# Layer 1's attention in other turns: sums of weights on quarter columns, byte masks, results turned back together

## The chip, the cores and the metric

The kernel runs on one core of one Trainium2 chip. The metric is the device time of one execution in microseconds (us). A smaller time is better. The engines are TensorE (matrix products, PE in the profile; PEld is its loading of weights), VectorE (DVE), ScalarE (ACT), GpSimd (POOL) and SyncE (SP), which here only issues DMAs.

## What is computed

The reference takes `x` of 32 x 512 x 256 and an adjacency `adj` of 32 x 512 x 512 with entries 0 and 1, and applies two layers. Each layer is a graph step and a feed-forward step, both added to `x` after a layer norm. The change lies in the graph step of layer 1, an attention with 4 heads of 64 values:

```python
h = jnp.einsum('bnd,hde->bhne', nodes_embed, W)
e_src = jnp.einsum('bhne,hte->bhtn', h, a_src)
e_dst = jnp.einsum('bhne,hte->bhtn', h, a_dst)
for t in range(n_types):
    mask = (node_adj == t + 1).astype(h.dtype)[:, None]
    weight = weight + mask * (e_src[:, :, t, :, None] + e_dst[:, :, t, None, :])
weight = jax.nn.leaky_relu(weight, negative_slope=0.01)
weight = jnp.where(node_adj[:, None] == 0, NEG, weight)
attention = jax.nn.softmax(weight, axis=-1)
dst = jnp.einsum('bhij,bhje->bhie', attention, h) + bias[None, :, None, :]
out = jax.nn.relu(dst) + h
```

The result is normalised per head, scaled and added to `x`. The feed-forward step of layer 1, called the mixer below, weighs all tokens into 64 slices, runs a short scan over the slices and spreads the result back over the tokens.

## The kernel before

An image `b` (32 of them) has 512 tokens, in NT = 4 tiles of P = 128 tokens. AH = 4 heads form AP = 2 pairs `q`; HO = 64 values make up a head.

Layer 0 runs first and takes somewhat more than half of the time. Layer 1 (`layer1_plain`) has three parts as Python generators, which are advanced step by step, so that their instructions alternate in each engine's queue. The order in which instructions are issued is fixed at build time.

`prepare(b)` brings an image in. GpSimd gathers its rows into `x` (L1075; five buffers, so that it waits for the store of an image five before), SyncE loads the adjacency tile by tile (`ai`, L1084). ScalarE turns a tile into bf16 (`a`, L1092) and sums squares (L1093). `turn_edges` (L1146 on) transposes a tile on TensorE into PSUM (`maskp`) and VectorE copies it into `mask` (L1151). Then come the layer norm (`hv`), its transpose (`x3T`), the product with the weights (`hp`, L1121), and exponentials on ScalarE, which are finished so that attention needs only a maximum and a product. The terms of the other side are brought to all partitions by four DMAs into `own` (L1141).

`attention(b)` goes through eight turns, pair by pair and within a pair over the four tiles `j` of neighbours: (0,0), (0,1), (0,2), (0,3), (1,0) and so on. `weigh` makes a turn's two tiles of weights `att` on VectorE (L1160: the larger of `own` and `other`, times `mask`), three turns (AHEAD) before TensorE uses them. A turn then has four f32 matmuls (L1199), each with 512 moving elements per partition. Two of them multiply the two heads' values (`avp`): head k of the pair goes to PSUM partitions 64k to 64k+63, hence to that half of the array's columns. The other two multiply a column that holds a factor of the weights' sum, repeated 64 times, by the same weights (`adp`), again on half of the columns each. They give every head the sum it has to be divided by, 64 equal rows of it.

After a pair's last turn ScalarE copies `adp` and `avp` to SBUF (`adT`, `avT`, L1205 and L1206). `back` (L1169 on) transposes both, four 128 x 128 pieces each (`dp`, `bp`, L1175), and VectorE divides (`rs`, L1177 and L1178; `av`, L1179). For the first pair this comes one turn later, in the middle of the image. `norm` (L1228 on) does the per-head normalisation of an image during the first turns of the next.

The mixer `mixer(g)` takes a group of two images: `slices` (exponentials of `lgp`, sums `yTp`, transposes `swp`), `tokens` (`uTp`, `rnp`), `scan` (`xp`, `bcp`, `dtp`, `zp`, then `gp`, `segp`, `xtp`, `yp`, `qp`, `yTp`, `oTp`, `msp`, `vp`) and `unslice` (`outp`). Parts of these depend on one another in a chain over TensorE, VectorE and ScalarE.

Each `yield` of the mixer names how many steps of attention and preparation are wanted there. WANTED is the sum of these numbers over a group, TURNS and STEPS are the steps of one attention and of one preparation, and PACE is the number of steps given per wanted one. `woven` mixes an attention with the next image's preparation.

PSUM has two rings of four banks: "pv" for attention's results, "any" for everything else. The tiles `att`, `avT` and `adT` share one ring of ATT buffers.

Of the kernel before, what the change touches and what calls it, by code (L numbers as in the profile page):

```python
# [8 lines left out]
F32 = mybir.dt.float32  # L9
# [9 lines left out]
P = 128  # L19
N = 512  # L20
# [805 lines left out]
def layer1_plain(tc, ident, eps, x2s, ranks, adj, w, out, over, ps):  # L826
# [20 lines left out]
    SLOPE = 0.01  # L847
    HE = HO + 1
    AP = AH // 2
    TURNS = AP * (NT + 1) + 3  # L850
    STEPS = 15
    WANTED = 62
    AHEAD = 3
    ATT = 2 * (AHEAD + 2)
    AHEAD_X = 2 * GB + 1
    PACE = 1.04 * GB * (TURNS + STEPS) / WANTED

# [3 lines left out]
    with ExitStack() as ctx:  # L861
# [207 lines left out]
        def prepare(b):  # L1069

            while b >= AHEAD_X and b - AHEAD_X not in stored:
                yield True
            xt = xs[b] = sb.tile([P, NT, D], F32, tag="x", name=f"x{b}", bufs=AHEAD_X)
            for t in range(NT):
                nc.gpsimd.indirect_dma_start(  # L1075
                    out=xt[:, t, :], out_offset=None, in_=x2s[b // SEG],
                    in_offset=bass.IndirectOffsetOnAxis(
                        ap=ranks[:, b * NT + t : b * NT + t + 1].bitcast(U32), axis=0))

            a, raw = [], []  # L1080

            def load(t):
                raw.append(sb.tile([P, N], I32, tag="ai", name=f"ai{b}_{t}", bufs=2))
                nc.sync.dma_start(raw[t], adj[b, t * P : (t + 1) * P, :])  # L1084

            load(0)
            load(1)
            yield
            for t in range(NT):
                n = b * NT + t  # L1090
                a.append(sb.tile([P, N], BF16, tag="a", name=f"a{b}_{t}", bufs=3))
                nc.scalar.activation(a[t], raw[t], AF.Identity, accum_out=edges[:, 0, n : n + 1])  # L1092
                nc.scalar.activation(raw[t], raw[t], AF.Square, accum_out=edges[:, 1, n : n + 1])  # L1093
                if t + 2 < NT:
                    load(t + 2)
                if t == 1:
                    mask = sb.tile([P, NT, N], BF16, tag="mask", name=f"mask{b}")
                    yield
                if t:
                    turn_edges(b, t - 1, a[t - 1], mask)  # L1100
                    yield
                if t == 2:

                    hv = sb.tile([P, NT, AH, HE], F32, tag="hv", name=f"hv{b}")
                    xn = hv.rearrange("p t h e -> p (t h e)")[:, : NT * D].rearrange("p (t d) -> p t d", t=NT)
                    normed(xt, xn, f"c{b}")
                    nc.gpsimd.tensor_add(xt, xt, beta.unsqueeze(1).to_broadcast([P, NT, D]))
                    yield
            turn_edges(b, NT - 1, a[NT - 1], mask)
            yield  # L1110
            xnT = yield from turned(xn, "x3T", f"x3T{b}")
            yield


            ht = sb.tile([P, NT, AH * HO], F32, tag="ht", name=f"ht{b}")
            other = sb.tile([P, NT, AH], F32, tag="other", name=f"other{b}")
            mine = sb.tile([P, AH, NT], F32, tag="mine", name=f"mine{b}")
            for t in range(NT):
                ph = psum("any", f"hp{b}_{t}")
                for c in range(DC):  # L1120
                    nc.tensor.matmul(ph[:, : AH * (HO + 2)], xnT[:, c, t * P : (t + 1) * P], wa[:, c, :],  # L1121
                                     start=c == 0, stop=c == DC - 1)
# [12 lines left out]
            row = sb.tile([AH * NT, P], F32, tag="turned", name=f"turned{b}", bufs=1)  # L1135
            nc.scalar.copy(row, pt[: AH * NT, :P])
            own_row = dr.tile([AH, N], F32, tag="own", name=f"ownd{b}")
            nc.sync.dma_start(own_row.rearrange("h (t p) -> (h t) p", p=P), row)
            own = [wide("own", f"own{b}_{h}", AH + 1) for h in range(AH)]
            for h in range(AH):  # L1140
                nc.sync.dma_start(own[h], own_row[h].partition_broadcast(P))  # L1141
            for t in range(NT):
                nc.vector.tensor_mul(hv[:, t, :, :HO], hv[:, t, :, :HO], hv[:, t, :, HO:].to_broadcast([P, AH, HO]))
            ready[b] = mask, ht, hv, other, own
            yield
# [17 lines left out]
        def attention(b):  # L1163
# [1 line left out]
            mask, ht, hv, other, own = ready[b]  # L1165
            xt = xs[b]
            av = sb.tile([P, NT, AH, HO], F32, tag="av", name=f"av{b}", bufs=1)
            turns = [(q, j) for q in range(AP) for j in range(NT)]

            def back(q, vT, dT):  # L1170

                bt, dt = psum("pv", f"bp{b}_{q}"), psum("pv", f"dp{b}_{q}")
                for src, dst in ((dT, dt), (vT, bt)):
                    for t in range(NT):
                        nc.tensor.transpose(dst[:, t * P : (t + 1) * P], src[:, t * P : (t + 1) * P], ident)  # L1175
                rs = sb.tile([P, NT, 2], F32, tag="rs", name=f"rs{b}_{q}")
                nc.vector.tensor_scalar_max(rs, dt.rearrange("p (t h e) -> p t h e", t=NT, h=2)[:, :, :, 0], 1e-30)  # L1177
                nc.vector.reciprocal(rs, rs)  # L1178
                nc.vector.tensor_mul(av[:, :, 2 * q : 2 * q + 2, :], bt.rearrange("p (t h e) -> p t h e", t=NT, h=2),  # L1179
                                     rs.unsqueeze(3).to_broadcast([P, NT, 2, HO]))  # L1180

            def begin(b):
                if b < B and (b, 0, 0) not in weighed:
                    for q, j in turns[:AHEAD]:
                        weigh(b, q, j)

            begin(b)
            behind = None
            for i, (q, j) in enumerate(turns):
                if j == 0:  # L1190
                    pv, pd = psum("pv", f"avp{b}_{q}"), psum("pv", f"adp{b}_{q}")
                if i + AHEAD < len(turns):
                    weigh(b, *turns[i + AHEAD])

                for dst, col, n in ((pv, 0, HO), (pd, HO, 1)):
                    for k in range(2):
                        h = 2 * q + k
                        vals = hv[:, j, h, col : col + n]
                        nc.tensor.matmul(dst[k * HO : (k + 1) * HO, :], vals if n > 1 else vals.to_broadcast([P, HO]),  # L1199
                                         weighed[b, h, j], start=j == 0, stop=j == NT - 1)  # L1200
                for k in range(2):
                    weighed[b, 2 * q + k, j] = None
                if j + 1 == NT:
                    vT, dT = wide("att", f"avT{b}_{q}", ATT), wide("att", f"adT{b}_{q}", ATT)
                    nc.scalar.copy(dT, pd)  # L1205
                    nc.scalar.copy(vT, pv)  # L1206
                    behind = q, vT, dT
                yield
                if unfinished and i != 2:
                    next(unfinished[0], None)  # L1210
                    yield
                    if i > 2:
                        unfinished.pop()
                if j == 0 and behind:
                    back(*behind)
                    behind = None
                    yield
            if b + 1 in ready:
                begin(b + 1)
            back(*behind)  # L1220
            yield
            unfinished.append(norm(b, av))

        unfinished = []
# [37 lines left out]
        def slices(b, j, yT, rn):  # L1262
# [9 lines left out]
            nc.gpsimd.tensor_add(xt, xt, outb.unsqueeze(1).to_broadcast([P, NT, D]))  # L1272
            sw = sb.tile([P, NT, DI], F32, tag="sw", name=f"sw{b}", bufs=1)
            swT = sb.tile([P, KC, N], F32, tag="swT", name=f"swT{b}")
            yield 1
            for t in range(NT):
                pf = psum("any", f"lgp{b}_{t}")
                for c in range(DC):
# [45 lines left out]
        def scan(g, uT):  # L1324
# [120 lines left out]
            nc.vector.tensor_add(mix, mix, back)  # L1445
            nc.vector.tensor_mul(mix, mix, decay)

            yield 6
            py = psum("any", f"yp{g}")
            for j in range(GB):  # L1450
                half = slice(j * G, (j + 1) * G)
# [62 lines left out]
        def mixer(g):  # L1514
# [3 lines left out]
            sws = []  # L1518
            for j in range(GB):
                sws.append((yield from slices(g * GB + j, j, yT, rn)))  # L1520
            yield 2
            tokens(g, yT, rn, uT)
            v = yield from scan(g, uT)
            yield 2
# [656 lines left out]
```

## Time and profile before

Three runs took 4830.05, 4830.42 and 4847.82 us; the median is 4830.42. The profiled execution's span is 4838.2 us.

| Stretch (us) | length | TensorE busy | VectorE busy | ScalarE busy | GpSimd busy |
|---|---|---|---|---|---|
| 0 to 500 (layer 0) | 500 | 334 | 344 | 191 | 204 |
| 1500 to 2000 (layer 0) | 500 | 436 | 384 | 269 | 241 |
| 2600 to 2800 (layer 1 begins) | 200 | 168 | 143 | 97 | 68 |
| 3400 to 3600 (layer 1) | 200 | 190 | 144 | 95 | 51 |
| 4600 to 4838 (the end) | 238 | 200 | 119 | 81 | 30 |

Busy time is the time in which at least one instruction of the engine was under way. Some of the tiles and lines in layer 1, over the whole execution:

| Work | line | instructions | mean ns of one |
|---|---|---|---|
| matmul `avp` | L1199 | 1024 | 618 |
| matmul `adp` | L1199 | 1024 | 601 |
| weights `att` | L1160 | 512 | 801 |
| transposes `dp` / `bp` | L1175 | 256 / 256 | 275 / 273 |
| copies `adT` / `avT` | L1205, L1206 | 64 / 64 | 582 / 590 |

The profile shows each f32 matmul of the program as two instructions (a transpose as one); so 1024 instructions are 512 matmuls. A duration includes the way through the array, so that two instructions one after the other start closer together than their durations say. A line of a group reads: line, engine, operation, written tile <- read tiles, shape, number | busy us, mean ns | idle time of the engine just before them, and who ended it.

### The profile page before, as it was taken

How to read it: one execution, taken by the hardware profiler on the slowest of the kernel's cores; microseconds unless marked ns; L12 is line 12 of the kernel's file. 1: busy time of each engine (PE TensorE's matmuls, PEld its weight loads, DVE VectorE, ACT ScalarE, POOL GpSimd, SP SyncE). 2: the span in 40 equal slices, each digit the busy share in tenths (PEclk: the TensorE clock that was granted, in tenths of full speed). 3: DMA queues.
4: the chain of work that ended last, by engine and by line, in shares of the span. 5: the costliest groups of instructions: out<-in, count | busy, mean ns of one | idle time of the engine just before them, and what ended most of it. 6: DMA issues, size and time to landing. Idle time of an engine off the chain costs nothing.

```text
span 4838.2 us, 56908 instructions
## 1 busy us (share of the span) xinstructions
PE 4218.7 (87%) x19415; PEld 2599.7 (54%) x19415; DVE 3400.7 (70%) x7296; ACT 2327.8 (48%) x4852; POOL 1708.4 (35%) x2027
## 2 busy tenths in 40 slices
PE   5668888878888788878887999999999999999997
PEld 4545555555555555544554455555555555555555
DVE  6577777777777777767676876666777666676763
ACT  2335555455555455545555444444454344444432
POOL 2355344454444544443333222222222223222220
PEclk8889999999999999998998999999999999999998
DMA  4455343454434543354333111111111111111100
GB/s 120 155 172 173 128 133 131 138 186 132 132 124 130 197 137 115 128 202 144 123 126 102 49 51 53 44 53 44 40 49 42 49 51 53 53 44 48 43 9 19
DMA packets 235105, 474.13 MB, mean 98 GB/s; under 512 B 38300, under 2 KB 114076, under 8 KB 234805
## 3 DMA queue, kind: packets, MB, share of 16 engines
q0 software_dynamic: 80256, 282.38, 17.7%
q1 hardware_dynamic: 154548, 188.02, 12.1%
q8 instruction: 155, 2.54, 0.2%
q14 instruction: 146, 1.19, 0.1%
HBM read 413.16 MB, written 57.16 MB: 97 GB/s over the span
## 4 chain that ended last, share of the span: by engine, by line
PE 39%; DVE 18%; POOL 12%; issue 11%; DMA 7%; ACT 5%; SPq 0%; POOLq 0%; DVEq 0%; ACTq 0%
POOL rows L564 5%; DMA rows<-table,xs 4%; PE po L616 4%; PE clsp L589 3%; PE adp L1199 3%; PE avp L1199 3%; PE lgp L1279 3%; PE outp L1508 3%; DVE att L1160 3%; PE gatep L589 2%; DVE acc L603 2%; PE hp L1121 2%; PE yTp L1291 2%; POOL xs L531 2%; POOL x L1075 1%
## 5 line engine op out<-in xcount | busy, mean ns | idle before, releaser
L589 PE MATMUL clsp<-xnT,wc 128*128 128x512 f32 x1024 | 534.1, 636 | 51.6 <-ACT cls L591 40.3
L564 POOL DMA_INDIRECT rows<-table,xs x332 | 411.6, 1240 | 301.7 <-ACT best L568 218.7
L589 PE MATMUL gatep<-xnT,wg 128*128 128x512 f32 x1024 | 500.7, 605 | 11.1 <-ACT gate L591 10.8
L616 PE MATMUL po<-wd,acc 128*128 128x256 f32 x2048 | 476.5, 389 | 10.8 <-DVE acc L607 6.1
L616 PEld LDWEIGHTS po<-wd,acc 128*128 128x128 f32 x2048 | 396.2, 195 | 103.2 <-issue 25.0
L603 DVE SCALAR_TENSOR_TENSOR acc<-past,fld,acc 128x512 f32<-128x512 f32 x448 | 345.7, 776 | 92.4 <-ACT past L602 82.0
L1160 DVE SCALAR_TENSOR_TENSOR att<-own,other,mask 128x512 f32<-128x512 f32 x512 | 389.2, 801 | 9.5 <-DMA own<-ownd 6.4
L1199 PE MATMUL avp<-att,hv 128*64 128x512 f32 x1024 | 358.9, 618 | 5.2 <-DVE att L1160 4.7
L1199 PE MATMUL adp<-att,hv 128*64 128x512 f32 x1024 | 358.7, 601 | 0.0
L570 DVE SCALAR_TENSOR_TENSOR best<-rows,xs,best 128x1024 f32<-128x1024 f32 x212 | 264.9, 1282 | 118.5 <-DMA rows<-table,xs 82.8
L531 POOL DMA_INDIRECT xs<-rows_of,order x128 | 140.3, 1096 | 550.3 <-DVE acc L605 134.5
L412 PE MATMUL pm<-h,adj 128*128 128x257 f32 x1024 | 275.5, 408 | 66.9 <-DVE u L409 25.2
L1279 PE MATMUL lgp<-wsl,x4T 128*128 128x512 f32 x512 | 270.4, 663 | 53.7 <-ACT x4T L1064 52.8
L589 PEld LDWEIGHTS gatep<-xnT,wg 128*128 128x128 f32 x1024 | 196.0, 196 | 222.3 <-issue 181.3
L596 PE MATMUL tz<-ident,best 128*128 128x128 f32 x1024 | 180.9, 292 | 133.4 <-DVE best L570 74.7
L602 ACT ACTIVATE past<-tz,fld 128x512 f32<-128x512 f32 x448 | 289.0, 689 | 8.5 <-DVE acc L603 8.0
L598 ACT ACTIVATE acc<-tz,fld 128x512 f32<-128x512 f32 x256 | 198.2, 774 | 192.3 <-PE po L616 98.8
L589 PEld LDWEIGHTS clsp<-xnT,wc 128*128 128x128 f32 x1024 | 188.0, 200 | 180.3 <-issue 104.7
L596 PEld LDWEIGHTS tz<-ident,best 128*128 128x128 f32 x1024 | 131.5, 148 | 274.7 <-issue 132.1
L568 ACT ACTIVATE best<-rows,xs 128x1024 f32<-128x1024 f32 x120 | 135.3, 1144 | 298.5 <-DMA rows<-table,xs 298.5
L412 PEld LDWEIGHTS pm<-h,adj 128*128 128x128 f32 x1024 | 198.0, 203 | 131.8 <-DVE u L409 39.1
L591 ACT ACTIVATE gate<-gatep,fld 128x512 f32<-128x512 f32 x256 | 175.1, 684 | 145.8 <-PE gatep L589 139.4
(596 smaller groups left out, 9140.6 us busy)
## 6 DMA issues: line engine op xcount, KB each, us to landing
adji<-in_adj SPq DMA_DIRECT2D x128, 256.0 KB, 2.8
ai<-in_adj SPq DMA_DIRECT2D x128, 256.0 KB, 2.7
own<-ownd SPq DMA_DIRECT2D x128, 256.0 KB, 3.7
rows_of<-keep SPq DMA_DIRECT2D x32, 550.0 KB, 3.6
x<-in_x SPq DMA_DIRECT2D x32, 512.0 KB, 4.3
x2s<-xs SPq DMA_DIRECT2D x32, 512.0 KB, 2.9
out<-x SPq DMA_DIRECT2D x32, 512.0 KB, 3.3
rows<-table,xs POOLq DMA_INDIRECT x332, 5.5
```

The costliest lines, as they stand in the source:

```text
L412: nc.tensor.matmul(pm[:, : D + 1], a[:, i, t * P : (t + 1) * P], h[:, i, :], start=i == 0, stop=i == NT - 1)
L531: nc.gpsimd.indirect_dma_start(out=xg[:, t, :], out_offset=None, in_=rows_of[s], in_offset=bass.IndirectOffsetOnAxis(ap=order[:, s * ST + ...
L564: nc.gpsimd.indirect_dma_start(out=row, out_offset=None, in_=table, in_offset=bass.IndirectOffsetOnAxis(ap=idxs[:, k : k + 1].bitcast(U32) ...
L570: nc.vector.scalar_tensor_tensor(m, row, vals[:, k : k + 1], m, ALU.add, ALU.max)
L589: nc.tensor.matmul(pf, wf[:, c, f * P : (f + 1) * P], xnT[:, c, :], start=c == 0, stop=c == DC - 1)
L596: nc.tensor.transpose(pt[:, t, :], best[t][:, f * P : (f + 1) * P], ident)
L602: nc.scalar.activation(r, z, AF.Relu, bias=fld[:, f, AT + b : AT + b + 1])
L603: nc.vector.scalar_tensor_tensor(y, r, fld[:, f, CH + b : CH + b + 1], y, ALU.mult, ALU.add)
L616: nc.tensor.matmul(po[:, :D], acc[f][:, t * P : (t + 1) * P], wd[:, f, :], start=f == 0, stop=f == FC - 1)
L1160: nc.vector.scalar_tensor_tensor(e, own[h], other[:, j, h : h + 1], mask[:, j, :], ALU.max, ALU.mult)
L1199: nc.tensor.matmul(dst[k * HO : (k + 1) * HO, :], vals if n > 1 else vals.to_broadcast([P, HO]), weighed[b, h, j], start=j == 0, stop=j == ...
L1279: nc.tensor.matmul(pf, xnT[:, c, t * P : (t + 1) * P], wsl[:, c, :], start=c == 0, stop=c == DC - 1)
```

## The change

Inside an image the turns now go by tiles of neighbours first: (0,0), (1,0), (0,1), (1,1) and so on. Both pairs' values are gathered at once, in two PSUM banks. After both pairs of a tile `j`, four matmuls form the four heads' sums, each on 32 columns: head h goes to PSUM partitions 32h to 32h+31 of one bank. After the last turn the bank of sums and the two of values are copied; the sums are transposed once for all four heads, then the values of each pair, and VectorE forms the reciprocals for all heads in one instruction.

Weights are made two turns before their use instead of three, and this lead runs on into the next image, if that is ready. The masks are stored as bytes instead of bf16. A tile of the adjacency is transposed two tiles after it was loaded, instead of one. `own` gets one more buffer, the ring of ATT buffers has 11 instead of 10, and the numbers of the pacing are set to the new count of steps; three of the mixer's yields ask for one step more.

```diff
-    TURNS = AP * (NT + 1) + 3
+    TURNS = AP * NT + 6
-    WANTED = 62
-    AHEAD = 3
-    ATT = 2 * (AHEAD + 2)
+    WANTED = 66
+    AHEAD = 2
+    ATT = 2 * (AHEAD + 2) + AP + 1
+    HW = P // AH
...
-                    mask = sb.tile([P, NT, N], BF16, tag="mask", name=f"mask{b}")
+                    mask = sb.tile([P, NT, N], mybir.dt.uint8, tag="mask", name=f"mask{b}")
                     yield
-                if t:
-                    turn_edges(b, t - 1, a[t - 1], mask)
+                if t > 1:
+                    turn_edges(b, t - 2, a[t - 2], mask)
                     yield
...
-            turn_edges(b, NT - 1, a[NT - 1], mask)
-            yield
+            for t in range(NT - 2, NT):
+                turn_edges(b, t, a[t], mask)
+                yield
...
-            own = [wide("own", f"own{b}_{h}", AH + 1) for h in range(AH)]
+            own = [wide("own", f"own{b}_{h}", AH + 2) for h in range(AH)]
...
-            turns = [(q, j) for q in range(AP) for j in range(NT)]
+            turns = [(q, j) for j in range(NT) for q in range(AP)]
...
+            for n in range(AHEAD):
+                begin(b, n)
+            pv = [psum("pv", f"avp{b}_{q}") for q in range(AP)]
             for i, (q, j) in enumerate(turns):
-                if j == 0:
-                    pv, pd = psum("pv", f"avp{b}_{q}"), psum("pv", f"adp{b}_{q}")
                 if i + AHEAD < len(turns):
-                    weigh(b, *turns[i + AHEAD])
-
-                for dst, col, n in ((pv, 0, HO), (pd, HO, 1)):
-                    for k in range(2):
-                        h = 2 * q + k
-                        vals = hv[:, j, h, col : col + n]
-                        nc.tensor.matmul(dst[k * HO : (k + 1) * HO, :], vals if n > 1 else vals.to_broadcast([P, HO]),
-                                         weighed[b, h, j], start=j == 0, stop=j == NT - 1)
+                    begin(b, i + AHEAD)
+                elif b + 1 in ready:
+                    begin(b + 1, i + AHEAD - len(turns))
+
                 for k in range(2):
-                    weighed[b, 2 * q + k, j] = None
...
+                    h = 2 * q + k
+                    nc.tensor.matmul(pv[q][k * HO : (k + 1) * HO, :], hv[:, j, h, :HO], weighed[b, h, j],
+                                     start=j == 0, stop=j == NT - 1)
+
+                if q + 1 == AP:
+                    if j == 0:
+                        pd = psum("pv", f"adp{b}")
+                    for h in range(AH):
+                        nc.tensor.matmul(pd[h * HW : (h + 1) * HW, :], hv[:, j, h, HO:].to_broadcast([P, HW]),
+                                         weighed.pop((b, h, j)), start=j == 0, stop=j == NT - 1)
...
+            dT = wide("att", f"adT{b}", ATT)
+            nc.scalar.copy(dT, pd)
+            vT = [wide("att", f"avT{b}_{q}", ATT) for q in range(AP)]
+            for q in range(AP):
+                nc.scalar.copy(vT[q], pv[q])
+            yield
+            dt = back(dT, "dp")
+            rs = sb.tile([P, NT, AH], F32, tag="rs", name=f"rs{b}")
...
-            yield 1
+            yield 2
...
-            yield 6
+            yield 7
...
-            yield 2
+            yield 3
```

More of the change, by code (lines that the diff above doesn't have):

```diff
@@ L1167, in attention @@
             av = sb.tile([P, NT, AH, HO], F32, tag="av", name=f"av{b}", bufs=1)
-            turns = [(q, j) for q in range(AP) for j in range(NT)]
[L1170 to L1188, printed above, removed]
+            turns = [(q, j) for j in range(NT) for q in range(AP)]
+            def begin(b, n):
+                q, j = turns[n]
+                if (b, 2 * q, j) not in weighed:
+                    weigh(b, q, j)
+            def back(src, kind):
+                dst = psum("pv", f"{kind}{b}")
+                for t in range(NT):
+                    nc.tensor.transpose(dst[:, t * P : (t + 1) * P], src[:, t * P : (t + 1) * P], ident)
+                return dst
@@ L1201, in attention @@
-                for k in range(2):
-                    weighed[b, 2 * q + k, j] = None
[L1203 to L1207, printed above, removed]
+                    begin(b, i + AHEAD)
+                elif b + 1 in ready:
+                    begin(b + 1, i + AHEAD - len(turns))
+                for k in range(2):
+                    h = 2 * q + k
+                    nc.tensor.matmul(pv[q][k * HO : (k + 1) * HO, :], hv[:, j, h, :HO], weighed[b, h, j],
+                                     start=j == 0, stop=j == NT - 1)
@@ L1213, in attention @@
                         unfinished.pop()
[L1214 to L1220, printed above, removed]
-            yield
+            dT = wide("att", f"adT{b}", ATT)
[3 more added lines that the diff above has]
+                nc.scalar.copy(vT[q], pv[q])
+            yield
+            dt = back(dT, "dp")
+            rs = sb.tile([P, NT, AH], F32, tag="rs", name=f"rs{b}")
+            nc.vector.tensor_scalar_max(rs, dt.rearrange("p (t h e) -> p t h e", t=NT, h=AH)[:, :, :, 0], 1e-30)
+            nc.vector.reciprocal(rs, rs)
+            for q in range(AP):
+                bt = back(vT[q], f"bp{q}_")
+                heads = slice(2 * q, 2 * q + 2)
+                nc.vector.tensor_mul(av[:, :, heads, :], bt.rearrange("p (t h e) -> p t h e", t=NT, h=2),
+                                     rs[:, :, heads].unsqueeze(3).to_broadcast([P, NT, 2, HO]))
+                yield
             unfinished.append(norm(b, av))
```

## The prediction

> **What bounds the kernel now.** I read the page first: busy shares and the slices. The change touches only layer 1's attention, so I then took the table by stage for the stretch in which attention runs beside the mixer, the groups of instructions by shape in the same stretch, TensorE's own waits there, and last a timeline of one attention turn.
>
> ```profile
> PE 4218.7 (87%) x19415; PEld 2599.7 (54%) x19415; DVE 3400.7 (70%) x7296; ACT 2327.8 (48%) x4852; POOL 1708.4 (35%) x2027
> PE   5668888878888788878887999999999999999997
> ...
> 2800.00:4600.00 1800.00, 1692.41 (x9492) 1000.20 (x9489) 1240.37 (x2678) 834.07 (x2132) 489.73 (x373) 0.97 0.15 48
> ```
>
> The last line is 1800 us of the steady state, columns PE, PEld, DVE, ACT, POOL, clock, DMA share, GB/s. TensorE is busy 94% there, VectorE 69%, ScalarE 46%: a microsecond of matmul removed is a microsecond of time, unless it was hiding something. Attention runs from 2652 to 4688 us, and the mixers of 16 groups take about 134 us each.
>
> ```profile
> L1199 PE MATMUL adp<-att,hv 128*64 128x512 f32 x928 | 324.4, 601 | 0.0
> L1199 PE MATMUL avp<-att,hv 128*64 128x512 f32 x928 | 322.9, 617 | 0.0
> L1160 DVE SCALAR_TENSOR_TENSOR att<-own,other,mask 128x512 f32<-128x512 f32 x462 | 352.9, 803 | 9.5 <-DMA own<-ownd 6.4 <-PE adp L1199 2.8
> L1151 DVE COPY mask<-maskp 128x512 bf16<-128x512 bf16 x112 | 44.3, 411 | 3.2 <-PE maskp L1150 3.2
> L1177 DVE TENSOR_SCALAR rs<-dp 128x8 f32<-128x8 f32 x59 | 9.6, 163 | 105.3 <-PE dp L1175 105.1
> ...
> PE lgp L1279 <- ACT x4T L1064: 52.1, 10, 6.4
> PE rnp L1313 <- DVE rn L1299: 20.7, 14, 1.7
> PE yp L1453 <- DVE mix L1446: 17.8, 15, 1.6
> ```
>
> Read here (2760 to 4690 us): the sums of the weights (`adp`) cost TensorE as much as the weighted values (`avp`). TensorE's idle time lies at three places of the mixer, once a group each: before `lgp`, `rnp`, `yp`. It never waits for attention's weights, and VectorE stands 105 us at the head of its queue for `dp`.
>
> ```profile
> 3607.71 0.64 PE L1199 MATMUL adp<-att,hv 128*64 128x512 f32 x1
> 3607.72 0.64 PE L1199 MATMUL avp<-att,hv 128*64 128x512 f32 x1
> 3608.19 0.59 PE L1199 MATMUL adp<-att,hv 128*64 128x512 f32 x1
> 3608.20 0.59 PE L1199 MATMUL avp<-att,hv 128*64 128x512 f32 x1
> 3608.72 0.49 PE L1121 MATMUL hp<-wa,x3T 128*128 128x264 f32 x1
> ```
>
> Start, duration. One matmul of the program appears as two instructions, 0.43 us apart in a run; two matmuls on different halves of the columns start 10 ns apart and run side by side. So a pair costs 2 x 0.427 = 0.854 us, and the visit to the split array took 3608.72 - 3607.71 = 1.01: 0.155 us more than the pair, for going in and out.
>
> **What the Trainium skill says.** "TensorEngine Tiling (Array Packing)", Available Configurations and Key Properties: with all 128 rows the array can be four tiles of 32 columns, tiles work independently, and a change of tiling mode drains the engine. The trace agrees for two tiles of 64 (the pairs, the 0.155 us); no run here shows four. "TensorE: Matmul & The Clock Gate", Part 3, gives 2.38x for three column tiles of 32 at 512 elements: not full, but wider than two. "VectorE: DVE Perf Modes", What auto-detection actually checks: the doubled rate for a PSUM source needs every tensor 16-bit; the mask copy's 411 ns against 682 of `av<-bp,rs`, also 512 elements from PSUM, agrees, and byte masks give that up.
>
> **The change, part by part.** I counted the consecutive attention matmuls in the compiled TensorE order of both programs, since other work stands between them and a matmul left alone has no partner.
>
> - Column work. Before: 1024 matmuls in 245 runs; each run priced by its fuller half at 0.854 a matmul: 462.9 us. After: 512 on halves and 512 on quarters, in 180 runs that fall into 375 stretches of one width; with quarters four side by side: 360.4. Saved 102.5 us. Without breaks in the runs it would be 128 x 0.854 = 109.
> - Switches. Before 245 x 0.155 = 38.0. After 180 x 0.155 plus 195 changes between halves and quarters, for which the trace has no price: nothing at the least, 0.155 at most (a full drain and return); I take half, 0.08: 27.9 + 15.6 = 43.5. Costs 5.5 (from a gain of 10 to a loss of 20).
> - Turning back together: per image 12 transposes instead of 16. Four `dp` take 0.43 us, so 4 x 32 x 0.108 = 13.8 us off TensorE. One 512-wide ScalarE copy (0.58) fewer per image, 19 us of an engine at 46%: nothing. VectorE loses half of its `rs` instructions (163 + 195 ns x 32 = 11 us) and, more important, the stop for `dp` in the middle of an image: at 3604.8 it stood 2.6 us there with `mix`, which `yp` waits for, behind it.
> - Byte masks: 128 copies of 411 ns go to some 680 (bounds: 0 and 0.27 us each), so 35 us more of VectorE, hidden under its 31% idle, in an image's preparation, four at a time. The product `att` has f32 operands beside the mask; I put no change on it (minimum 692 ns, as other three-operand work).
> - Order: turns by j then pair, two ahead instead of three, weights of the next image drawn through its predecessor's last turns. The sixth `own` buffer and masks at half size touch no wait above 6.4 us. Edges turned two tiles behind instead of one, the normalisation of the next image one step earlier: same instructions, same DMAs (SP's `ai` and `own` loads, POOL's gathers) in the same number. The pacing figures (14 turns, 66 wants) only follow the new count of steps; attention still runs 4% ahead.
>
> TensorE work saved: 102.5 - 5.5 + 13.8 = 110.8 us, 6.9 a group.
>
> What comes back as idle. In the compiled order, attention pieces that stood in the mixer's gaps are gone, in each group. (1) Between `qp` and `yTp` stood `hp` and two pieces (1.0 us); now only `hp`, 1.9 us, against four VectorE steps of `y` that took 2.5 (3615.75 to 3618.16): +0.6. (2) Between `yTp` and `oTp` stood a pair (1.0) covering the copy of `yT` (0.59 plus hand-over); now at most one `minep` of 0.27: +0.7. (3) Between `msp` and `vp` stood one unpaired sum (0.9) over the copy of `oT`: +0.4. (4) Before `uTp`/`rnp` stands one pair instead of two: +0.9. (5) Before `yp` some 2.4 us of pieces are gone, but so is VectorE's 2.6 us stop: -0.3. (6) Weights: VectorE makes a turn's two in 2 x 0.743 = 1.49 us (median), TensorE now uses them in 0.854 + 0.427 + switches = 1.36 to 1.44 instead of 1.71; in bursts of three or four turns the lead of two runs out: I take +0.5. Together 2.8 a group, 45 us in all; from 20 (VectorE's freed queue repays more) to 80 (the weights starve each burst).
>
> Sum against the profiled span: 4838.2 - 110.8 + 45 = 4772. The other runs' median, 4830.4, lies 8 lower; the same saving gives 4764.
>
> The wait at `lgp`, 5 us a group, stays: it follows from the store of the image before, POOL's four gathers of 1.0 us into the same buffer, their landing and the `hv` normalisation, which stands before the exponentials in ScalarE's queue in both orders.
>
> **The rivals.**
> - Four wide and little given back: the 102.5 us counted whole, idle only 10 to 20: about 4735. For it: VectorE is relieved of its stops. Against: gaps (1) to (4) have nothing else to fill them.
> - Four wide, but VectorE and the mixer's chains become the bound: idle of 100 or more, time about 4825, no measurable change. For it: VectorE's product is 2 x 0.74 a turn and slower when POOL works (803 mean, 2845 the longest). Against: 69% busy leaves 560 us in 1800.
> - The quarters run two at a time only. Then each quad costs 1.71 us, 128 x 0.854 = 109 more: TensorE work comes to 469.8 + 43.5 - 13.8 = 499.5 against 500.9 before, nothing is saved, and the 37 us of lost fill (1 to 5) remain: 4866, slower. It decides from a quad of 1.37 us on: 128 x 0.51 less leaves a saving of 45, what comes back. For it: no matmul of this trace runs more than two wide, and four streams of f32 are read at once. Against: the skill's three tiles, and two f32 streams that lose nothing. Issue is no bar: `yp` issues 32 loads and 32 matmuls in 1.87 us, 29 ns each, and a quad of 16 instructions needs 0.47.
> - The sums could cease to be what they are: no, 32 equal rows instead of 64, read as one column.
>
> **How the numbers follow.** Likeliest, 0.60: 4764, its own range 4739 to 4799 (80 to 20 us given back, read from the median). Little given back, 0.17: 4700 to 4740. Given back whole, 0.10: 4806 to 4850. Two wide, 0.13: 4850 to 4890. A change under 0.5% (24 us) can't be told from none in this kernel: faster 0.77, same 0.10, slower 0.13. The range 4695 to 4835 leaves out the two-wide case and part of the third.
>
> **What would show it.** In the profile after: four `adp` instructions starting within some 30 ns and the next four 0.43 us later (right), or two and two (the slow rival). Busy time of `adp` near 170 us instead of 359. TensorE's idle time before `yTp`, `oTp`, `vp` and `rnp` up by about 2.6 us a group; waits of `avp` for `att` of some 8 us. The mask copy near 0.68 us. VectorE's wait for `dp` halved. I am wrong if quads take over 1.4 us, if TensorE's busy share falls under 88% between 2800 and 4500 us, or if the wait at `lgp` moves by more than 2 us a group.

## The result, and the profile after

The changed kernel took 4759.24 us (median of four runs, 4757.25 to 4776.06), against 4833.78 for the kernel before beside it. The ratio is 0.985, interval 0.982 to 0.988: 1.5% faster, 74.5 us. The forecast was 4764. The profiled execution was the slowest of the four: span 4774.3.

First two lines of the page, then the stretch from 2800 to 4600 us, in the columns used for the kernel before:

```profile
PE 4124.6 (86%) x19287; PEld 2525.6 (53%) x19287; DVE 3414.5 (72%) x7232; ACT 2308.9 (48%) x4820; POOL 1713.8 (36%) x2027
PE   5667888888898888987899798999999999999987
...
2800.00:4600.00 1800.00, 1673.86 (x9883) 975.87 (x9881) 1319.77 (x2776) 856.64 (x2193) 519.40 (x386) 0.98 0.16 49
```

TensorE is busy 94 us less over the execution, and 93% instead of 94% in the steady stretch; VectorE has risen from 69% to 73%. The groups by shape (2760 to 4620 us):

```profile
L1162 DVE SCALAR_TENSOR_TENSOR att<-own,other,mask 128x512 f32<-128x512 f32 x468 | 334.3, 738 | 23.8 <-DMA own<-ownd 23.7
L1195 PE MATMUL avp<-att,hv 128*64 128x512 f32 x936 | 267.1, 613 | 0.0
L1202 PE MATMUL adp<-att,hv 128*32 128x512 f32 x942 | 132.9, 604 | 0.0
L1153 DVE CAST mask<-maskp 128x512 uint8<-128x512 bf16 x112 | 75.9, 678 | 8.5 <-PE maskp L1152 8.5
L1218 DVE TENSOR_SCALAR rs<-dp 128x16 f32<-128x16 f32 x30 | 5.1, 168 | 1.8 <-PE dp L1181 1.7
```

`adp` now stands for 133 us where it stood for 324 (over the whole execution 150 for 359). A mask copy takes 678 ns instead of 411. VectorE's wait for `dp` has all but gone (105 to 1.7 us). How the quarters run is seen in the timeline of TensorE (start, duration, number of instructions):

```profile
3570.76 1.08 PE L1195 MATMUL avp<-att,hv 128*64 128x512 f32 x4
3571.77 1.06 PE L1202 MATMUL adp<-att,hv 128*32 128x512 f32 x8
3572.76 1.94 PE L1195 MATMUL avp<-att,hv 128*64 128x512 f32 x8
3574.63 1.06 PE L1202 MATMUL adp<-att,hv 128*32 128x512 f32 x8
3575.62 0.64 PE L1195 MATMUL avp<-att,hv 128*64 128x512 f32 x1
```

Eight instructions of four heads' sums take 0.99 us from start to start, where one pair of matmuls took 0.854. So all four run side by side, and 0.14 is left for the change of width. Two pairs of `avp` take 1.87 against 2 x 0.854, again 0.16 over. A change between halves and quarters therefore costs about as much as going in and out of the split array (0.155), not half of it.

TensorE's own waits have moved altogether (2810 to 4600 us; waiting instruction, who released it, us in total, times, longest). Before these were `lgp`, `rnp` and `yp`:

```profile
PE yTp L1295 <- DVE sw L1290: 38.1, 27, 2.4
PE yTp L1295 <- DVE mask L1153: 33.7, 5, 7.5
PE lgp L1283 <- DVE mask L1153: 15.3, 13, 3.4
PE oTp L1480 <- ACT yT L1474: 10.4, 14, 1.3
PE yTp L1472 <- DVE y L1467: 8.2, 10, 0.9
PE hp L1123 <- ACT x3T L1065: 5.7, 11, 1.6
PE vp L1502 <- ACT oT L1483: 1.7, 5, 0.3
```

TensorE's granted clock has to be read with them. One wait at `lgp` in the kernel before, first ScalarE, then TensorE, then the stretch just after (its third number from the end is the clock):

```profile
3521.30 2.07 ACT L1054 ACTIVATE hv<-x,shiftc,rsc 128x256 f32<-128x256 f32 x4 [5.60 <-DVE shiftc L1052]
3523.28 0.56 ACT L1064 COPY x4T<-x4T12p 128x512 f32<-128x512 f32 x1
3523.89 3.78 PE L1279 MATMUL lgp<-wsl,x4T 128*128 128x512 f32 x4 [5.41 <-ACT x4T L1064]
3530.03 1.94 PE L1279 MATMUL lgp<-wsl,x4T 128*128 128x512 f32 x4
3522.00:3528.00 6.00, 4.11 (x8) 1.86 (x9) 5.92 (x7) 2.73 (x6) 5.06 (x5) 0.50 0.29 87
```

The copy of `x4T` stands in ScalarE's queue behind the normalisation `hv` of the next image, which waits for its `shiftc`. TensorE waits 5.4 us, and then the clock is 0.50 for a while: four instructions of `lgp` take 3.78 us, later 1.94. From start to start they need 854 ns there and 429 ns elsewhere. Each of the ten waits of this kind in the stretch (4.8 to 6.4 us) is followed by half clock, which sets in 2.2 to 4.2 us after the wait began; so are the four waits of 7.5 us at `yTp` in the changed kernel, while waits of some 2 us are followed by it only in part. That the wait causes it was not tested by itself. Between 2810 and 4600 us the clock is halved for 113 us before and for 58 after.

To compare kernels I use the length of a group: the start of the last group's `xp` less that of the first's, by 15. TensorE's busy share between 2810 and 4600 us splits it into busy and idle time. Of the busy time I count half of what lies in stretches of half clock as lost to the clock, and the rest as work. This split is an estimate: it takes all of TensorE's work to be slowed as `lgp` is.

| Kernel | first / last `xp` (us) | a group | TensorE busy | clock | work | lost to the clock | idle |
|---|---|---|---|---|---|---|---|
| before | 2779 / 4770 | 132.8 | 1683.43 of 1790 | 0.97 | 121.5 | 3.3 | 7.9 |
| after | 2800 / 4704 | 126.9 | 1663.86 | 0.98 | 116.4 | 1.6 | 8.9 |
| sums on halves (first experiment) | 2790 / 4714 | 128.3 | 1718.58 | 0.99 | 122.1 | 1.1 | 5.1 |
| lead at the end (below) | 2798 / 4755 | 130.5 | 1625.87 | 0.96 | 115.7 | 2.8 | 12.0 |

Tenths of the work are not to be read closely: kernels with the same matmuls in another order (the changed one, the lead at the end, the three additions below) lie between 115.1 and 116.4.

### The profile page after: what moved, and what is told of

Its sections match the earlier page's. It is cut to its first block, busy times and chain, and to the rows that moved or that the text cites. A ratio compares the mean times of both kernels' runs of the same rounds, so it can differ in the third digit from the quotient of the medians.

```text
span 4774.3 us, 56581 instructions
## 1 busy us (share of the span) xinstructions
PE 4124.6 (86%) x19287; PEld 2525.6 (53%) x19287; DVE 3414.5 (72%) x7232; ACT 2308.9 (48%) x4820; POOL 1713.8 (36%) x2027
## 4 chain that ended last, share of the span: by engine, by line
PE 30%; DVE 22%; POOL 12%; issue 10%; DMA 8%; ACT 8%; SPq 0%; POOLq 0%; DVEq 0%; ACTq 0%
POOL rows L564 4%; DMA rows<-table,xs 4%; PE po L616 4%; PE clsp L589 3%; DVE att L1162 3%; PE gatep L589 3%; PE avp L1195 2%; DVE acc L603 2%; DVE sw L1285 2%; POOL x L1076 2%; PE outp L1512 2%; PE hp L1123 2%; POOL xs L531 1%; PE yTp L1295 1%; PE oTp L1480 1%
## 5 line engine op out<-in xcount | busy, mean ns | idle before, releaser
L1162 DVE SCALAR_TENSOR_TENSOR att<-own,other,mask 128x512 f32<-128x512 f32 x512 | 364.7, 738 | 23.8 <-DMA own<-ownd 23.7
L1295 PE MATMUL yTp<-sw,x 128*128 128x512 f32 x512 | 254.3, 637 | 79.9 <-DVE sw L1290 41.8
L1195 PE MATMUL avp<-att,hv 128*64 128x512 f32 x1024 | 295.4, 617 | 4.1 <-DVE att L1162 4.1
L1283 PE MATMUL lgp<-wsl,x4T 128*128 128x512 f32 x512 | 245.0, 611 | 19.9 <-DVE mask L1153 15.3
```

The costliest lines, as they stand in the source:

```text
L1162: nc.vector.scalar_tensor_tensor(e, own[h], other[:, j, h : h + 1], mask[:, j, :], ALU.max, ALU.mult)
L1195: nc.tensor.matmul(pv[q][k * HO : (k + 1) * HO, :], hv[:, j, h, :HO], weighed[b, h, j], start=j == 0, stop=j == NT - 1)
L1283: nc.tensor.matmul(pf, xnT[:, c, t * P : (t + 1) * P], wsl[:, c, :], start=c == 0, stop=c == DC - 1)
L1295: nc.tensor.matmul(py, xn[:, t, c * P : (c + 1) * P], sw[:, t, :], start=t == 0, stop=t == NT - 1)
```

## The experiments

Ratios below are to the kernel before, run beside each. Where a time is compared with the changed kernel, the latter's ratio is 0.985; a repeat gave 0.986 (0.984 to 0.989), see the second experiment. In the diffs `...` marks what is left out.

**Sums on halves again, all else changed.**

```diff
-                        pd = psum("pv", f"adp{b}")
+                        pd = [psum("pv", f"adp{b}_{r}") for r in range(AP)]
                     for h in range(AH):
-                        nc.tensor.matmul(pd[h * HW : (h + 1) * HW, :], hv[:, j, h, HO:].to_broadcast([P, HW]),
+                        r, k = divmod(h, 2)
+                        nc.tensor.matmul(pd[r][k * HO : (k + 1) * HO, :], hv[:, j, h, HO:].to_broadcast([P, HO]),
...
```

The lines left out copy the two banks of sums and transpose them pair by pair, so that TensorE has as many matmuls as before.

> The changed kernel, but the four sums on halves of the columns again (two banks, 64 rows each, transposed pair by pair); order of turns, masks, lead and pacing stay changed. Theory of the prediction (the quarters are the gain): TensorE gets 109 us of column work and 13.8 us of transposes back and loses some 27 us of switches, so the gain is gone: 4820 to 4860 us. Rival (the order of turns and VectorE's missing stop for dp are the gain): 4760 to 4790 us, TensorE just busier.

Measured: 4791.15 us, ratio 0.991 (0.989 to 0.993). My theory asked for 4820 to 4860 and misses; the rival's 4760 to 4790 is nearer. The repeat of the changed kernel in the same series took 4772, so the quarters are worth about 19 us. The table says why. With the transposes that they spare they do take TensorE's work away, 5.7 us a group, but idle time grows by 3.8 and the loss to the clock by 0.5. And the other edits have already gained 48 us without taking work away (122.1 against 121.5): idle time is 2.8 us a group less, and the loss to the clock 2.2. The waits in this kernel (same stretch):

```profile
PE yTp L1299 <- DVE sw L1294: 34.8, 26, 2.5
PE x3T13p L1064 <- DVE mask L1153: 4.3, 1, 4.3
...
PE lgp L1287 <- DVE mask L1153: 3.0, 5, 1.1
```

The waits at `lgp`, `rnp` and `yp`, 88 us before in this stretch, are down to some 7, without the quarters.

**GpSimd's addition of the output bias moved, in both kernels.**

```diff
-            nc.gpsimd.tensor_add(xt, xt, outb.unsqueeze(1).to_broadcast([P, NT, D]))
...
             nc.vector.reciprocal(rn[:, j, :], rn[:, j, :])
+            nc.gpsimd.tensor_add(xt, xt, outb.unsqueeze(1).to_broadcast([P, NT, D]))
             return swT
```

> The changed kernel with GpSimd's addition of the output bias to x moved from before the logits to after the slices' last transposes. Theory (a VectorE instruction that meets a GpSimd addition of 1024 elements is stretched by 2 us, and in the changed kernel that is the product sw, which yTp waits for): no stretched sw product (21 before), TensorE's wait of yTp for sw from 42 us to under 20, time 10 to 30 us less than the changed kernel: 4730 to 4750. Rival (the stretched instruction hides, or the collision only moves to another instruction that matters as much): 4752 to 4770.

> The kernel before with the same move of GpSimd's bias addition. Theory of the collision (before, the addition stretches mix, which yp waits for): the step mix+back from 2.4 to 0.7 us each time, TensorE's wait at yp from 18 to under 8 us, time 5 to 15 us below the kernel before. Rival, the prediction's (VectorE's stop for dp of the first pair holds up mix): mix gets shorter, but the wait at yp stays above 13 us and the time within 4 us of before.

Measured: 4771.97 us, ratio 0.986 (0.984 to 0.989), and 4842.11, ratio 1.001 (1.000 to 1.002). Both experiments tell nothing of their question. The compiled order of instructions turned out to be that of the unmoved kernel on every engine: place in the source does not decide where an instruction goes here. They are repeats of the two kernels, and show how well such ratios repeat: to 0.2%.

**The adjacency turned one tile behind its load.**

```diff
-                if t > 1:
-                    turn_edges(b, t - 2, a[t - 2], mask)
+                if t:
+                    turn_edges(b, t - 1, a[t - 1], mask)
...
-            for t in range(NT - 2, NT):
-                turn_edges(b, t, a[t], mask)
-                yield
+            turn_edges(b, NT - 1, a[NT - 1], mask)
+            yield
```

> The changed kernel with the adjacency turned one tile behind its load, as before. Theory (the lag of two tiles and the earlier normalisation have little effect beside the rest, as the prediction's zero for them says): within 10 us of the changed kernel, 4750 to 4770; the wait of 5 us a group stays away from lgp or comes back with the waits at yTp gone. Rival (the lag of two is what took away the wait at lgp): lgp waits for x4T 40 us or more again and the time is 4780 to 4810. Second rival (the lag costs at the start of layer 1): the first attention begins 5 to 10 us earlier after layer 0's end than in the changed kernel, and the time falls to 4745 to 4752.

Measured: 4753.47 us, ratio 0.984 (0.981 to 0.986): no difference from the changed kernel that can be told. `lgp` does not wait for `x4T` again, so the lag did not take that wait away, and the first `xp` comes 172 us after layer 0's last `po`, in the changed kernel 173. The zero for this edit holds.

**GpSimd's two additions to `x` tile by tile.**

```diff
-                    nc.gpsimd.tensor_add(xt, xt, beta.unsqueeze(1).to_broadcast([P, NT, D]))
+                    for i in range(NT):
+                        nc.gpsimd.tensor_add(xt[:, i, :], xt[:, i, :], beta)
...
-            nc.gpsimd.tensor_add(xt, xt, outb.unsqueeze(1).to_broadcast([P, NT, D]))
+            for i in range(NT):
+                nc.gpsimd.tensor_add(xt[:, i, :], xt[:, i, :], outb)
```

> The changed kernel with GpSimd's two additions to x (beta, output bias) as four instructions of 256 elements each instead of one of 1024. Theory (a VectorE instruction that meets a GpSimd addition is stretched until that one ends, and TensorE pays for it at yTp): no VectorE product sw above 1.6 us (21 of about 2.7 us in the changed kernel), TensorE's waits of yTp for sw from 42 us to about 25, time 5 to 20 us below the changed kernel. Rival (the stretch is hidden elsewhere, or four pieces catch VectorE more often): within 5 us of it, or slower.

Measured: 4759.26 us, ratio 0.984 (0.983 to 0.986). The mechanism is there. VectorE's product of the slices, first in the changed kernel, then here (duration in ns: least / median / most):

```profile
L1285 DVE TENSOR_TENSOR sw<-sw,ebsl x128: 636/684/2952, 2727.9 to 4689.3; 128x512 f32<-128x512 f32 x128
```

```profile
L1287 DVE TENSOR_TENSOR sw<-sw,ebsl x128: 631/684/1549, 2711.2 to 4662.2; 128x512 f32<-128x512 f32 x128
```

TensorE's wait of `yTp` for `sw` fell from 38.1 to 14.8 us. But its wait at `yp` rose from 1.3 to 12.3, and the time is at most 10 us lower, within what the repeats differ by.

**Mask copies on ScalarE.**

```diff
-            nc.vector.tensor_copy(mask[:, :, t * P : (t + 1) * P], pt)
+            nc.scalar.copy(mask[:, :, t * P : (t + 1) * P], pt)
```

> The changed kernel with the 128 mask copies (0.68 us each) on ScalarE instead of VectorE. Theory (with the quarters VectorE has become TensorE's equal as the bound; most of the quarters' saving comes back as waits for it): VectorE loses 87 us, TensorE's waits for mask and sw (91 us in the changed kernel) halve, time 15 to 40 us less: 4720 to 4750. Rival (TensorE's work still sets the time, the waits only move): within 8 us of the changed kernel. Second rival (ScalarE's queue stands behind the normalisation hv, so the masks come later): slower by 5 to 30 us.

Measured: 4779.59 us, ratio 0.988 (0.986 to 0.990). TensorE's waits for the masks are gone, but those of `yTp` for `sw` have risen from 38 to 88 us:

```profile
PE yTp L1295 <- DVE sw L1290: 88.4, 51, 4.2
```

VectorE stands at 68% here (1215.91 of 1790 us) and is waited for more. So less work on VectorE alone does not help. That ScalarE's queue delays the exponentials, as the second rival has it, is in the trace in part: on the mean of the stretch an exponential starts 1.63 us after its `lgp` ended, in the changed kernel 1.29, but VectorE's product, too, starts 2.96 us after the exponential instead of 2.69. Which of the two makes the loss is not shown.

**The new pacing alone in the kernel before.**

```diff
-    WANTED = 62
+    WANTED = 66
...
-            yield 1
+            yield 2
...
-            yield 6
+            yield 7
...
-            yield 2
+            yield 3
```

> The kernel before with the three larger yields of the mixer and 66 wants, nothing else. The prediction's theory (the pacing figures only follow the count of steps): within 6 us of before, waits at lgp, rnp and yp as before (52, 21, 18 us). Rival (the pacing is what took the waits at lgp and rnp away): 20 to 45 us faster than before, wait at lgp under 20 us.

Measured: 4863.62 us, ratio 1.005 (1.003 to 1.006): slower by 24 us, where nothing was forecast and the rival had a gain. The waits at `lgp` (40 us) and `rnp` (18) stay.

**Both pairs turned back at the image's end, in the kernel before** (with byte masks, and two more `att` buffers).

```diff
...
-                if j == 0 and behind:
-                    back(*behind)
-                    behind = None
-                    yield
...
-            back(*behind)
-            yield
+            for part in behind:
+                back(*part)
+                yield
```

> The kernel before with the first pair's results kept and turned back at the end of the image with the second's, and byte masks to make room for the two tiles this holds. Theory (VectorE's stop for dp in the middle of the image delays mix and rn, for which TensorE waits): VectorE's wait for dp from 105 us to under 60, TensorE's waits at yp and rnp together from 38 us to under 15, time 10 to 30 us below before. Rival (the turns' new order or the wait at lgp is the source of the gain at unchanged TensorE work): time within 6 us of before.

Measured: 4864.3 us, ratio 1.005 (1.004 to 1.007). VectorE does not stop for `dp` any more, and `yp` does not wait (16 us before). Whether the stop had held `mix` up is still open: a collision with GpSimd that had made `mix` longer (last section) is gone in this kernel too. `rnp` still waits 19 us, `lgp` now 81, and the time is longer by 24 us.

**The three additions by tile, edges one tile behind.** GpSimd's two additions to `x` by tile and the adjacency turned one tile behind, as above, and the attention's bias (L1132) by tile too.

```diff
-            nc.gpsimd.tensor_add(hv[:, :, :, :HO], ht.rearrange("p t (h e) -> p t h e", h=AH),
-                                 abias.rearrange("p (h e) -> p h e", h=AH).unsqueeze(1).to_broadcast([P, NT, AH, HO]))
+            for t in range(NT):
+                nc.gpsimd.tensor_add(hv[:, t, :, :HO], ht[:, t, :].rearrange("p (h e) -> p h e", h=AH),
+                                     abias.rearrange("p (h e) -> p h e", h=AH))
```

> The changed kernel with GpSimd's three additions (beta, output bias, and the attention's bias in L1132) by tile, and the adjacency turned one tile behind its load: the two edits that cost nothing alone, and VectorE's wait for the attention's bias cut too. Theory (VectorE's standing is now what TensorE pays for): VectorE's wait of hv for GpSimd from 123 us to under 60, TensorE's waits at yTp under 30 us, time 15 to 35 us below the changed kernel: 4725 to 4745. Rival (TensorE's order sets the time, the waits move on): within 8 us of the changed kernel.

Measured: 4745.86 us, ratio 0.981 (0.980 to 0.983), 0.4 to 0.5% below the changed kernel. VectorE's wait for the attention's bias fell from 123 to 72 us, short of the 60 expected; TensorE waits 41 us at the two `yTp` (80 before the edits), but 21 at `lgp` for `sw` and 12 at `yp`. Part of the gain moved on, as the rival said.

**The next image's first weights made after the last turn.**

```diff
-                elif b + 1 in ready:
-                    begin(b + 1, i + AHEAD - len(turns))
...
+            if b + 1 in ready:
+                for n in range(AHEAD):
+                    begin(b + 1, n)
```

> The changed kernel with the first weights of the next image made together after an image's last turn, as before, instead of one turn at a time beside the last turns. Theory (the lead running on through the border is what took the waits at lgp and rnp away): they come back, 20 us or more of each, time 20 to 45 us more than the changed kernel. Rival (the new order of turns, both pairs of a tile together, does it): within 8 us.

Measured: 4822.9 us, ratio 0.996 (0.995 to 0.997): three quarters of the gain lost by this edit. But not where I put it. `lgp` and `rnp` do not wait again; `yTp` does:

```profile
PE yTp L1296 <- DVE mask L1153: 71.6, 10, 7.9
PE yTp L1296 <- DVE sw L1291: 43.6, 19, 6.6
PE lgp L1284 <- DVE mask L1153: 15.6, 13, 3.6
```

Idle time rises from 8.9 to 12.0 us a group and the loss to the clock from 1.6 to 2.8; the work does not grow. The likely reason is that four weights in one lump stand in VectorE's queue at the end of each image, where `mask` and `sw` are wanted: for the last tile of an image the product `sw` starts 6.25 us after its exponential, in the changed kernel 3.04.

**The old pacing in the changed kernel** (yields 1, 6 and 2, 62 wants; the diff above, backwards).

> The changed kernel with the pacing's old yields (1, 6, 2) and 62 wants. The prediction's theory (pacing follows only the count): within 8 us of the changed kernel. Rival (pacing and the new turns belong together: alone the pacing cost the kernel before 0.5%): 15 to 40 us slower, with waits at lgp or at yp of 20 us or more. Second rival (it is a plain cost in both): 15 to 25 us faster.

Measured: 4746.77 us, ratio 0.980 (0.979 to 0.982). The second rival is right: the new pacing costs some 20 us in either kernel. It was not run together with the additions by tile.

**The lead running on, in the kernel before** (three turns, byte masks, two more `att` buffers).

```diff
                 if i + AHEAD < len(turns):
                     weigh(b, *turns[i + AHEAD])
+                elif b + 1 in ready:
+                    weigh(b + 1, *turns[i + AHEAD - len(turns)])
...
```

> The kernel before with its lead of three turns running on into the next image turn by turn, and byte masks for the room of two more tiles. Theory (the lead takes the waits at lgp, rnp and yp away): their sum from 91 us to under 50 and the time 20 to 45 us below before. Rival (the order of turns does): time within 10 us of before, the waits stay. Byte masks alone cost 35 us of VectorE and by either theory no time.

Measured: 4867.02 us, ratio 1.006 (1.004 to 1.008). `lgp` waits 32 us instead of 53 and never for `x4T`, but 17 us of these are for `mask` (before 0.7), transposes of masks now wait 27 us for ScalarE, and TensorE's idle sum is 111 us against 107. No gain: what is worth 1% in the new order of turns is worth nothing here. Byte masks were never tried alone in the kernel before, and both kernels that had them there lost 24 to 26 us; so a gain of this edit, or of the turning back at the end, may be hidden behind a loss by the masks.

## Why the prediction was right, and where not

The time and the total are right: 110.8 saved and 45 given back were expected, 66 in all; the profiled spans differ by 64, the timed medians by 74.5. That the quarters run four wide is right too. But part by part the terms are less good, and that the total agrees so well is partly luck.

- TensorE's work. Expected 6.9 us less a group. Busy time falls by just that, from 124.9 to 117.9, but 1.7 of it is time lost to the clock, of which the prediction says nothing. The work falls by 5.1. The quarters, as wide as the likeliest case had them, save 5.7 together with the transposes that they spare, near the 6.0 that the numbers expected for the first experiment come to; the slow rival falls. One term was too small: a change of width was taken at 0.08 us and costs 0.14 to 0.16. On 195 changes that is 12 to 16 us, up to 1.0 a group. The rest of the difference stays open.
- Idle time that comes back. Expected 2.8 us a group, measured 1.0 in the steady state. Of the six items, two have the right size: the wait at the mixer's scan `yTp` (+0.6 expected; 8.2 us over 14 groups is 0.6) and at `oTp` (+0.7; 10.4 over 14 is 0.7). `vp` was put at 0.4 and came to 0.1. `rnp` was put at +0.9 and fell from 1.4 to 0.1. `yp` was put at -0.3 and fell by 1.1. For weights (+0.5) no matmul `avp` waits in the steady state at all.
- The wait at `lgp` was said to stay, 5 us a group. It came less often than the prediction reads: ten waits in some 14 groups, 52 us, are below 4 a group. And the step that it would stay failed, by the criterion set for it: all waits at `lgp` together fell from 53 to 18 us in the stretch. The reason given was that the normalisation `hv` stands in ScalarE's queue before the exponentials in both orders. What counts is whether it stands before the copies of `x4T`, as in the lines above. In the kernel before it stands between the two copies in 10 of 32 images; in the changed one in none. There it stands behind both copies in 28 images, in 14 of them still before the exponentials. So `lgp` can start, and what comes later is `sw`. Its place was taken by a wait that the prediction does not list: `yTp` of the slices, for `sw` and `mask`, 72 us or 5 a group.
- The sum. The listed gains and losses in part cancel. A group is 5.9 us shorter, where 4.1 were expected; that makes 88 us on 15 groups. Against it stand 11 us more from layer 0's last `po` to the first `xp` (173 instead of 162), 3 more at the end, and 11 by which layer 0, where nothing was changed, ended later in this execution; unrounded, 64 are left. The start was not foreseen; byte masks or the longer lag may do it, but the lag undone still gives 172, and the two kernels with the old order and byte masks, with 173 and 176, differ in more than that.
- So the reason given, TensorE's work, holds for the quarters and is misleading for the whole. The first experiment takes the quarters away and loses 19 us, not 60 to 100. The order of turns and its company remove 2.8 us of idle time a group and 2.2 of loss to the clock; the quarters then remove 5.7 us of work, of which 3.8 are waited away and 0.5 lost to the clock. The two-wide rival was mis-priced by the same step: as far as the first experiment stands for it, the kernel without the quarters' saving is 1% faster, not slower, since its 37 us of lost fill do not arise.
- Which edit moved the normalisation, and so ended the wait at `lgp`, is known only by elimination. Undoing the lag of the edges, the pacing, the quarters or the running lead, each alone in the changed kernel, does not bring it back. In the old order the running lead takes the wait for `x4T` away as well, without a gain. Byte masks and the turning back at the end leave it in place there. What remains is the new order of turns with the sums last, the lead of two instead of three, the sixth `own` buffer, or several edits together. These were not separated.
- Costed at nothing: the lag of the edges, rightly; the pacing, wrongly (some 20 us slower in both kernels); the lead across the border, wrongly: without it 51 us (4823 against 4772, the repeat) of the gain are lost.

## What to carry to other kernels

Where the bounding engine is 94% busy, a saving of its work is not yet a saving of time: put work, time lost to a lower clock and idle time apart, stage by stage, and ask whom the engine will wait for once it is faster. Here 5.7 us a group saved on TensorE gave 1.4, and an edit that saves no work at all, the weights made one turn at a time over the border of two images, was worth 50 us. What an edit is worth beside others need not show when it is tried in the old order: there the running lead, with byte masks, came out slower.

## What the runs showed of the hardware

Four f32 matmuls on 32 columns each, with 128 rows and 512 moving elements, run side by side at the pace of one: 0.99 us for four, of which 0.14 is the change of width; the four start within 20 ns of one another. The Trainium skill, "TensorE: Matmul & The Clock Gate", Part 3, gives 2.38x for three column tiles of 32 with 512 elements; here four give 4 x 0.854 / 0.99 = 3.5x, with the change of width counted. No run here has three.

A VectorE instruction with two tensors in SBUF that starts about when a GpSimd addition does, or during it, ends only after it. This held for all 21 products `sw<-sw,ebsl` that met one in the changed kernel. One of them:

```profile
3647.81 2.95 DVE L1285 TENSOR_TENSOR sw<-sw,ebsl 128x512 f32<-128x512 f32 x1
3647.88 2.33 POOL L1108 TENSOR_TENSOR x<-x,beta 128x1024 f32<-128x1024 f32 x1
```

The product takes 684 ns otherwise. The Trainium skill, "SBUF — State Buffer", Who interferes with whom, says that an instruction with two SBUF inputs contends with a GpSimd instruction that reads SBUF. The trace agrees, and adds the price: 2.3 us for an addition of 1024 elements. `av<-bp,rs`, with one of its two tensors in PSUM, met an addition 15 times in the kernel before and never took over 0.70 us. Which instruction is hit is a matter of the order. In the kernel before it was `mix` in 14 of 16 groups, in the changed one never. The step as it stands before, and then after:

```profile
L1445 DVE TENSOR_TENSOR mix<-mix,back 128x512 f32<-128x512 f32 x16 | 38.8, 2427 | 0.1
```

```profile
L1449 DVE TENSOR_TENSOR mix<-mix,back 128x512 f32<-128x512 f32 x16 | 11.1, 691 | 0.5
```

The prediction explains the wait at `yp` by VectorE's stop for `dp` alone. The collision stood beside it. In the kernel before with the new pacing, `mix` is stretched in five groups, and in just these `yp` waits 1.1 to 1.2 us; of the other eleven, eight do not wait at all. But in the five the stop for `dp` is 2.6 us, in the eight 1.3. So the end of the collision very likely helped to end the wait; the runs do not separate it from the stop, since the move meant to test it did not change the order.
